# A macaron block on one core: the attention's table of steps made anew, with explicit lists for its first and last turns

## The chip, the cores and the metric

The kernel runs on one core of a Trainium2 chip. The metric is the device time of one execution in microseconds; the median over several runs is compared. The profile is of one execution, and its times are counted from the start of its span.

## What is computed

A block of three layers on `x` of shape (8, 1024, 256), float32: half a mixture-of-experts feed-forward layer, a memory layer called attention, and the same feed-forward layer again, each on the layer-normalised input and added to it.

```
x = x + 0.5 * ffn(layernorm(x))      # 8 experts, top-1, relu, weighted by the softmax
x = x + attn(layernorm(x))
x = x + 0.5 * ffn(layernorm(x))

# attn, for each batch row, in chunks of 128 tokens:
k, v, q = causal_conv4(x @ Wk.T), causal_conv4(x @ Wv.T), causal_conv4(x @ Wq.T)
alpha, eta, theta = means of sigmoid / sigmoid / softplus of three projections
g = grad of sum((silu(k @ W1.T) @ W2.T - v)**2) at the chunk's first W1, W2, clipped by its norm
S = eta_t * S - theta_t * g_t ;  W = (1 - alpha_t) * W + S        # for each token t
h = silu(q_t @ W1_t.T) ;  r_t = h @ W2_t.T
out = rmsnorm(r @ Wo.T) * norm_g * (x @ gW.T + gb)
```

The memory `W1, W2, S` goes from chunk to chunk, so that the eight chunks form a chain; all else of a chunk depends on its own tokens (and three tokens of the chunk before, for the convolution).

## The kernel before

The first expert layer, the attention and the second expert layer follow one another in `macaron`. In the attention a chunk `c` holds 128 tokens of all 8 batch rows, and there are `NC` = 8 chunks. The work of a chunk is cut into named steps, the methods of the class `Memory`. A step with `yield` in it comes in several pieces, one for each engine that it passes: `zk`, for instance, is a product on PE (L866), a sigmoid on ACT (L889) and a product on DVE (L891).

The pieces of a chunk, in the order of its data:

- The input. `load` (L640) fetches half of the rows through ACT's DMA queue into one of three buffers; `lx` (L645, DVE), `norm` (POOL, L627 to L653) and `xn` (L658, ACT) normalise them; `turn` (L665, L669) transposes them by PE and copies them by ACT.
- The projections, all on PE into two `pre` banks of PSUM. `ae` and `aem` give alpha and eta, `few` (L704, SP's queue) gathers them in eight rows, `prods` (L710, DVE) and `cut` (L719, POOL) finish these, and `spread` (L725 to L734, SP's queue) spreads them over the partitions by way of DRAM. `proj0`, `proj1`, `proj2` are k, v, q (L755; ACT copies L784, L787), `tap0` to `tap8` (L791, DVE) their convolution. `theta`, `soft`, `softplus`, `thm` give theta. `lt` and `ct` (L710, DVE) are the scans of the decay factors over time, 128 x 1024. `rows` transposes k and v, `qk` and `mq` (L850) weigh q by k.
- The gradient, which needs the chunk's memory. `zk` (L866, L889, L891) applies W1, `pred` (L876, L879, L866, L905) W2, `back` (L876, L879, L866, L912) goes back; `ds`, `sq`, `kn`, `both`, `clip` (L929 to L939, with a power on POOL, L95) give the clipped factor, `gc0` and `gc1` (L944, DVE) the scaled gradients.
- The next memory. `old0` to `old3` (L959 to L965, POOL) scale the old one, `step0`, `step1` (L977, PE) sum the gradients, `state` (L986, DVE) adds both, `by_out` (L995, L1004) transposes it.
- The output. `rq`, `hq`, `abh`, `hh`, `rh`, `rts` (L1014 to L1076) read the memory by q, `wide` (L1107, L1114) is the product with Wo and its squares, `rms` (POOL, L1121, L1122), `gate` (L1091, PE; L1099, ACT), `xo` (L1129, DVE), `add` (L1135, POOL, adds the residual row that `xr` fetched through ACT's queue, L1082), and `store` (L1140) sends two copies of 512 KB through ACT's queue. The output buffer `xo` exists twice, so a product of L1129 waits until the store that used its buffer two halves ago has left it.
- The routing of the second expert layer. `lo`, `std` (L102 to L107, POOL), `back_turn` (L1160, L1162), `logits` (L1169, L1179, L1182, L1185), and at the last chunk `choose`.

Every engine runs its instructions in the order in which the program issues them (`manual_schedule`), and that order is the table `ORDER`. A turn goes through the table once. `step-1` in it means that the step is done for the chunk before the one that the turn is named after, `step+1` for the chunk after it; a name that occurs again stands for the step's next piece. Turns before the first and after the last chunk use the same table and leave out what falls outside the eight chunks:

```
for turn in range(-max(offs), NC - min(offs)):
    for name, n, off in order:
        c = turn + off
        if not 0 <= c < NC:
            continue
```

In the table of before, the input of a chunk is turned and projected in the turn in which its `zk`, `pred` and `back` begin, `back` ends in the next turn (`rq-1`, `gc0-1`, `state-1`), and the outputs of a chunk come one and two turns later.

Of the kernel before, what the change touches and what calls it, by code (L numbers as in the profile page):

```python
# [1226 lines left out]

def attention(sh, i, x1, x2, out):
    nc, tc = sh.nc, sh.tc
    words = [re.fullmatch(r"([a-z_]+?)(\d*)([+-]\d)?", s).groups() for s in ORDER.split()]  # L1230
    order = [(name, int(n or 0), int(off or 0)) for name, n, off in words]
    offs = [off for _, _, off in order]
    with ExitStack() as st:
        mem = Memory(st, sh, i, x1, x2, out)
        begun = {}
        st.enter_context(tc.manual_schedule(engines=sh.engines))
        for turn in range(-max(offs), NC - min(offs)):
            for name, n, off in order:
                c = turn + off
                if not 0 <= c < NC:  # L1240
                    continue
                key = name, n, c
                if key in begun:
                    next(begun[key], None)
                    continue
                g = getattr(mem, name)(c, mem.u[c], n)
                if g is not None:
                    begun[key] = g
                    next(g, None)
# [72 lines left out]
```

## Time and profile before

| | |
|---|---|
| time, median of 3 runs | 820.73 us (820.3 to 824.27) |
| the profiled execution | 824.22 us, of which its span 822.4 us |
| mean granted PE clock | 0.927 |
| busy over the span: PE, DVE, ACT, POOL | 740.3, 453.8, 346.7, 470.6 us |
| the attention, first `xn` to last logit of the routing | 231.7 to 639.6 us |
| the state updates (L986), chunks 1 to 7 | begin at 284.7, 326.8, 373.7, 419.6, 466.1, 511.9, 561.8 us |
| the first product with the state (`zk`, L866), chunks 0 to 7 | begins at 252.4, 289.9, 331.6, 378.2, 424.0, 470.7, 516.5, 566.4 us |

Busy time is the union of an engine's records. PE's matmuls are pipelined and their ends are modelled, so that a PE that is busy all the time need not run at its peak. A line of a timeline gives the start in us, the duration in us (of a run of like instructions, from the first to the last), the engine, the line of the kernel, the operation with output and inputs, and in brackets how long the engine had been idle before it, and which producer ended that. A row of a table of stretches gives each engine's busy time in that stretch, the number of its instructions in brackets, then the granted PE clock (1.00 is full speed), the share of the DMA engines that was busy, and their GB/s. A line of the waits gives who waited for whom: us in total, times, and the longest.

### The profile page before, as it was taken

How to read it: one execution, taken by the hardware profiler on the slowest of the kernel's cores; microseconds unless marked ns; L12 is line 12 of the kernel's file. 1: busy time of each engine (PE TensorE's matmuls, PEld its weight loads, DVE VectorE, ACT ScalarE, POOL GpSimd, SP SyncE). 2: the span in 40 equal slices, each digit the busy share in tenths (PEclk: the TensorE clock that was granted, in tenths of full speed). 3: DMA queues.
4: the chain of work that ended last, by engine and by line, in shares of the span. 5: the costliest groups of instructions: out<-in, count | busy, mean ns of one | idle time of the engine just before them, and what ended most of it. 6: DMA issues, size and time to landing. Idle time of an engine off the chain costs nothing. (4 is left out here: it accounts for less than half of the span.)

```text
span 822.4 us, 13632 instructions
## 1 busy us (share of the span) xinstructions
PE 740.3 (90%) x5198; PEld 540.6 (66%) x5198; DVE 453.8 (55%) x931; ACT 346.7 (42%) x738; POOL 470.6 (57%) x610
## 2 busy tenths in 40 slices
PE   7869999999568999999999989999885599999996
PEld 5547777777426575766768575766663377777775
DVE  5862333220328988888887878868643534322310
ACT  3512222222047575767666676756433122222221
POOL 6625444531134768988888888875754354444411
PEclk9959999999867999999999999889968589999999
DMA  8995444540214242454454442334306824444420
GB/s 265 367 386 166 151 138 150 172 152 17 88 52 84 79 93 90 91 169 102 157 129 129 130 123 85 85 121 106 129 26 194 279 74 138 138 144 138 145 70 17
DMA packets 110945, 110.40 MB, mean 134 GB/s; under 512 B 12384, under 2 KB 103904, under 8 KB 110880
## 3 DMA queue, kind: packets, MB, share of 16 engines
q1 hardware_dynamic: 72528, 66.49, 27.1%
q10 hardware_dynamic: 32464, 31.47, 12.2%
q0 software_dynamic: 5888, 11.57, 4.3%
q8 instruction: 41, 0.67, 0.3%
q14 instruction: 24, 0.20, 0.1%
HBM read 78.80 MB, written 30.64 MB: 133 GB/s over the span
## 5 line engine op out<-in xcount | busy, mean ns | idle before, releaser
L352 ACT ACTIVATE hT<-ph 128x320 f32<-128x320 f32 x128 | 56.0, 437 | 225.5 <-PE ph L345 225.5
L345 PE MATMUL ph<-xT,w1t 128*128 128x320 f32 x512 | 149.5, 446 | 0.8 <-ACT xT L306 0.8
L345 PEld LDWEIGHTS ph<-xT,w1t 128*128 128x128 f32 x512 | 96.6, 194 | 41.9 <-issue 4.5
L373 DVE SCALAR_TENSOR_TENSOR xo<-py,gate,xg 128x256 f32<-128x256 f32 x32 | 15.5, 484 | 187.2 <-PE py L366 187.2
L366 PE MATMUL py<-w2t,hT 128*128 128x256 f32 x512 | 114.6, 382 | 0.0
L366 PEld LDWEIGHTS py<-w2t,hT 128*128 128x128 f32 x512 | 96.1, 190 | 13.7
L277 POOL DMA_INDIRECT gate<-gate_d,get x48 | 45.4, 945 | 33.8 <-DMA gate_d<-gates 19.8
L1091 PE MATMUL pre<-wg,xT 128*128 128x256 f32 x256 | 60.1, 394 | 2.5 <-DVE m L850 2.0
L755 PE MATMUL pre<-xT,w 128*64 128x512 f32 x256 | 61.4, 603 | 0.5 <-ACT kk L787 0.5
L1091 PEld LDWEIGHTS pre<-wg,xT 128*128 128x128 f32 x256 | 49.4, 196 | 11.1 <-DVE m L850 2.4
L1135 POOL TENSOR_TENSOR xo<-xo,xr 128x512 f32<-128x512 f32 x32 | 42.9, 1353 | 20.4 <-DVE xo L1129 20.2
L376 POOL DMA_INDIRECT x<-xo,put x16 | 16.0, 1002 | 54.3 <-DVE xo L373 45.8
L658 ACT ACTIVATE xt<-xt,ln_nm,lx_t 128x256 f32<-128x256 f32 x64 | 34.4, 593 | 25.0 <-POOL ln_nm L653 25.0
L376 POOL DMA_INDIRECT out<-xo,put x16 | 16.0, 1003 | 48.0 <-DVE xo L373 36.6
L1129 DVE SCALAR_TENSOR_TENSOR xo<-tail,rs,gate 128x256 f32<-128x256 f32 x64 | 27.1, 476 | 25.1 <-DMA out<-xo 16.2
L944 DVE TENSOR_TENSOR gc<-ehd,c 128x1536 f32<-128x1536 f32 x16 | 40.0, 2539 | 0.3
L755 PEld LDWEIGHTS pre<-xT,w 128*64 128x64 f32 x256 | 15.8, 136 | 30.4 <-issue 22.4
L665 PE MATMUL pre<-ident,xt 128*128 128x128 f32 x128 | 21.5, 303 | 15.5 <-ACT xt L658 14.1
L856 POOL TENSOR_TENSOR abq<-qq,ab 128x512 f32<-128x512 f32 x16 | 33.6, 2103 | 1.0 <-DMA ab<-kept 1.0
L678 PE MATMUL pre<-xT,w 128*128 128x512 f32 x64 | 32.6, 640 | 0.0
L389 PE MATMUL py<-w2t,hT 128*64 128x128 f32 x512 | 31.5, 276 | 0.0
L266 POOL DMA_INDIRECT xg<-hidden_in,get x24 | 23.6, 984 | 13.2 <-issue 6.7
(252 smaller groups left out, 1573.5 us busy)
## 6 DMA issues: line engine op xcount, KB each, us to landing
w1t<-w_in SPq DMA_DIRECT2D x16, 1024.0 KB
w2t<-w_in SPq DMA_DIRECT2D x16, 1024.0 KB
xt<-hidden_in SPq DMA_DIRECT2D x16, 512.0 KB
x<-xt SPq DMA_DIRECT2D x16, 512.0 KB
xt<-x ACTq DMA_DIRECT2D x16, 512.0 KB
xr<-x ACTq DMA_DIRECT2D x16, 512.0 KB
x<-xo ACTq DMA_DIRECT2D x14, 512.0 KB
out<-xo ACTq DMA_DIRECT2D x14, 512.0 KB
```

Of the source, the lines that this page charges most:

```text
L277: nc.gpsimd.indirect_dma_start(out=gate[:, s : s + 1], out_offset=None, in_=slots.gate, in_offset=bass.IndirectOffsetOnAxis(ap=slots.get[: ...
L345: nc.tensor.matmul(ph[:, :CAP], lhsT=a[:, c, f * P : (f + 1) * P], rhs=at[:, c, :], start=(c == 0), stop=(c == 1),)
L352: nc.scalar.activation(hT[:, f, :], ph[:, :CAP], AF.Relu)
L366: nc.tensor.matmul(py[:, :H], lhsT=hT[:, f, s * P : (s + 1) * P], rhs=b[:, f, :], start=(f == 0), stop=(f == FC - 1),)
L376: nc.gpsimd.indirect_dma_start(out=dst, out_offset=bass.IndirectOffsetOnAxis(ap=slots.put[:, e, s : s + 1], axis=0), in_=xo[:, s, :], in_o ...
L658: self.nc.scalar.activation(x, x, AF.Identity, bias=u.nm[:, j : j + 1], scale=u.r16[:, j : j + 1])
L678: self.nc.tensor.matmul(ps, lhsT=self.w3[:, k, 4 * D : 6 * D], rhs=u.xT[:, k, h * 512 : (h + 1) * 512], start=(k == 0), stop=(k == 1),)
L755: self.nc.tensor.matmul(ps[self.half[r], :], lhsT=self.w3[:, k, f * D : (f + 1) * D], rhs=u.xT[:, k].rearrange("h (p r t) -> h p r t", p=N ...
L856: self.nc.gpsimd.tensor_tensor(u.abq[:, n], u.kv[2], u.ab[:, n], ALU.mult)
L944: self.nc.vector.tensor_tensor(u.gc[:, layer], g.unsqueeze(2).to_broadcast([P, B, 3, D]), u.c3.rearrange("s n j -> s j n").unsqueeze(3).to ...
L1091: self.nc.tensor.matmul(ps[:, q * H : (q + 1) * H], lhsT=u.xT[:, k, j * P : (j + 1) * P], rhs=self.wg[:, k, :], start=(k == 0), stop=(k == 1),
L1135: self.nc.gpsimd.tensor_tensor(u.xo[h][:, two], u.xo[h][:, two], u.xr[h][:, two], ALU.add)
```

## The change

The table `ORDER` is made anew, with 163 entries instead of 165, and it is used for the middle turns only. Two lists, `FIRST` (398 entries) and `LAST` (393), name each step with its chunk (`zk@1`). A new function `steps` unfolds the table as before, replaces as many entries at its beginning as `FIRST` has by `FIRST`, and those at its end by `LAST`; both lists hold exactly the entries that they replace, in another order. The steps themselves are not changed. In the new table the input of a chunk is turned and projected in the turn before its `zk` (`turn0+1`, `proj0+1`), `back`, `clip` and `gc` fall in the chunk's own turn, and the output's second half comes at the start of the turn after next.

```diff
 ORDER = """
-choose0-2 gate0-2 xn3 store1-3 mq1-1 rms0-2 gate1-2 sq0-1 gate2-2 back-1 xo0-2 abq0-1 sq0-1 gate1-2 xo1-2
-xr1-2 gate3-2 sq2-1 both-1 gate2-2 turn0 turn0 ends-1 gate3-2 kn-1 rq-1 sq2-1 add0-2 turn1 old0-1
-turn3 turn1 add1-2 load1+1 back_turn0-2 turn2 clip-1 clip-1 lx1+1 turn3 turn2 ae0 back_turn1-2 ae0
-lx0+1 ae1 lo0-2 old1-1 lo1-2 back_turn0-2 back_turn1-2 ae1 old2-1 old3-1 proj0 clip-1 load0+2 gc0-1
-std0-2 gc1-1 aem logits0-2 lx2+1 proj0 proj0 aem logits0-2 hq-1 lx3+1 tap0 tap1 step1-1 logits0-2
-few tap2 logits0-2 norm+1 hq-1 hq-1 proj1 step0-1 xr0-1 proj1 prods cut abh1-1 wide1-2 proj1 theta
-state-1 wide1-2 tap3 hh-1 proj2 rms1-2 theta tap4 hh-1 xo2-2 abh0-1 theta xn0+1 proj2 zk add2-2
-proj2 xo3-2 tap5 rh-1 add3-2 zk rows1 soft tap6 rows1 zk softplus lo2-2 pred rows0 lo3-2 pred
-back_turn2-2 back_turn2-2 spread tap7 back_turn3-2 rts-1 back_turn3-2 rts-1 ds pred std1-2 tap8
-logits1-2 rows0 logits1-2 by_out-1 kept lt logits1-2 ksq sq1 logits1-2 choose1-2 thm pred thm wide0-1 back
-past+1 xn1+1 ds by_out-1 abq1 back qk wide0-1 ct back mq0 xn2+1 gate0-1 sq1 store0-2
+prods step0-1 tap0 step1-1 hq-1 proj2 tap1 tap3 tap4 xo3-2 theta cut proj2 theta xo2-2 norm+1 add3-2
+gate3-1 tap2 theta add2-2 state-1 hq-1 lo3-2 hh-1 tap5 by_out-1 tap6 abh0-1 hh-1 store0-2 tap7 gate3-1
+abh1-1 xr1-1 spread soft softplus back_turn3-2 back_turn2-2 xr0-1 back_turn3-2 back_turn2-2 lo2-2 std1-2
+rows0 rows1 tap8 lt zk logits0-2 rows0 logits0-2 by_out-1 zk logits1-2 rh-1 xn1+1 kept thm rts-1
+logits1-2 logits1-2 thm zk rows1 pred ds abq0 sq1 logits1-2 pred ct qk ds mq0 pred rts-1 xn0+1 wide0-1
+pred wide0-1 mq1 ends rms0-1 ksq sq1 xn2+1 gate0-1 gate0-1 old1 gate1-1 past+1 gate2-1 xn3+1 back
+gate1-1 gate2-1 back turn0+1 turn0+1 turn1+1 load1+2 lx0+2 back xo0-1 xo1-1 sq0 turn1+1 add0-1 kn
+turn2+1 add1-1 back_turn1-1 sq0 back turn2+1 turn3+1 back_turn0-1 ae0+1 sq2 both turn3+1 ae0+1 ae1+1
+back_turn1-1 sq2 ae1+1 abq1 clip rq old0 back_turn0-1 logits0-1 aem+1 store1-2 lo1-1 lx1+2 proj0+1
+logits0-1 aem+1 lx2+2 few+1 lo0-1 proj0+1 proj0+1 wide1-1 clip proj1+1 proj2+1 old2 wide1-1 std0-1 clip
+gc0 load0+3 old3 proj1+1 hq proj1+1 rms1-1 gc1 lx3+2
 """
+FIRST = """
...
+proj0@0 aem@0 lx1@1 lx2@1 proj0@0 tap0@0 norm@1 load1@2 aem@0 few@0 proj1@0 proj1@0 proj1@0 prods@0
+xn1@1 theta@0 tap3@0 proj2@0 tap1@0 xn2@1 tap2@0 theta@0 cut@0 tap4@0 proj2@0 theta@0 zk@0 xn0@1 kept@0
+tap5@0 zk@0 zk@0 turn1@1 proj2@0 tap6@0 tap7@0 spread@0 pred@0 xn3@1 ds@0 ds@0 old1@0 turn3@1 turn1@1
+pred@0 turn3@1 rows0@0 rows0@0 turn2@1 turn2@1 rows1@0 rows1@0 turn0@1 load0@2 tap8@0 pred@0 lt@0
+turn0@1 sq1@0 qk@0 ct@0 soft@0 past@1 ksq@0 mq0@0 old0@0 ae1@1 ae1@1 mq1@0 pred@0 proj1@1 back@0 sq1@0
+proj1@1 proj1@1 ae0@1 sq0@0 lx2@2 load0@3 proj0@1 ae0@1 lx1@2 tap3@1 back@0 proj0@1 kn@0 proj0@1 proj2@1
+back@0 proj2@1 lx3@2 abq1@0 aem@1 sq0@0 both@0 lx0@2 proj2@1 tap0@1 gate3@0 softplus@0 old2@0 back@0
...
+back@1 ds@1 turn1@2 back@1 sq0@1 xo1@0 turn3@2 sq0@1 turn1@2 load1@3 xo0@0 lx0@3 sq1@1 back@1
...
+clip@1 soft@2 tap0@2 tap1@2 clip@1 proj2@2 std0@0 proj2@2 rms1@0 gc0@1 gc1@1 store0@0 hq@1 xo2@0 old3@1
+add2@0 prods@2 xo3@0 step1@1 gate0@1 step0@1 proj1@2 lx3@3 hq@1 gate0@1 cut@2 proj1@2 add3@0 softplus@2
+tap6@2 hq@1 back_turn2@0 spread@2 thm@2 lx2@3 tap7@2 state@1 proj1@2 hh@1 lo3@0 back_turn3@0
...
+"""
+LAST = """
...
+back@7 ds@7 abq0@7 sq1@7 gate1@6 rms0@6 xo0@6 back@7 ds@7 back@7 ends@7 gate2@6 sq0@7 kn@7 sq0@7
+both@7 gate1@6 step0@7 add0@6 back@7 xo1@6 sq2@7 logits1@5 thm@7 sq2@7 gate2@6 add1@6 thm@7 clip@7
+logits1@5 lo1@6 store1@5 back_turn0@6 back_turn1@6 clip@7 back_turn0@6 lo0@6 back_turn1@6 wide1@6 rq@7
+wide1@6 store0@6 std0@6 rms1@6 clip@7 gc0@7 hq@7 xo3@6 gate0@7 xo2@6 add3@6 hq@7 hq@7 add2@6 gate1@7
+logits0@6 back_turn3@6 gc1@7 lo3@6 old3@7 abh0@7 logits0@6 back_turn3@6 back_turn2@6 by_out@7 lo2@6 hh@7
+back_turn2@6 by_out@7 xr0@7 abh1@7 hh@7 logits1@6 rh@7 gate0@7 logits1@6 rts@7 store1@6 logits0@6
+logits0@6 logits1@6 std1@6 rts@7 logits1@6 xr1@7 wide0@7 gate3@7 gate1@7 wide0@7 rms0@7 xo0@7 add0@7
+gate3@7 xo1@7 choose0@7 wide1@7 add1@7 lo1@7 gate2@7 wide1@7 rms1@7 gate2@7 xo3@7 kept@7 xo2@7
+back_turn0@7 add3@7 lo0@7 back_turn0@7 back_turn1@7 back_turn1@7 logits0@7 store0@7 add2@7 logits0@7
+back_turn2@7 back_turn3@7 back_turn2@7 logits0@7 std0@7 back_turn3@7 lo3@7 lo2@7 logits0@7 logits1@7
+std1@7 store1@7 logits1@7 logits1@7 logits1@7 choose1@7
+"""
+
+
+def steps():
+
+    turn_of = [re.fullmatch(r"([a-z_]+?\d*)([+-]\d)?", s).groups() for s in ORDER.split()]
+    turn_of = [(name, int(off or 0)) for name, off in turn_of]
+    offs = [off for _, off in turn_of]
+    plan = [
+        (name, turn + off)
+        for turn in range(-max(offs), NC - min(offs))
+        for name, off in turn_of
+        if 0 <= turn + off < NC
+    ]
+    first, last = ([(s.split("@")[0], int(s.split("@")[1])) for s in t.split()] for t in (FIRST, LAST))
...
+    a, b = len(first), len(plan) - len(turns)
...
+    return first + plan[a:b] + last
 
 
 def attention(sh, i, x1, x2, out):
...
-        for turn in range(-max(offs), NC - min(offs)):
-            for name, n, off in order:
...
+        for step, c in steps():
...
```

More of the change, by code (lines that the diff above doesn't have):

```diff
@@ new lines @@
+gc0 load0+3 old3 proj1+1 hq proj1+1 rms1-1 gc1 lx3+2
+"""
+FIRST = """
+load0@0 load1@0 lx1@0 lx2@0 lx3@0 load0@1 lx0@0 norm@0 xn1@0 xn0@0 turn1@0 xn2@0 xn3@0 turn0@0 turn1@0
+turn0@0 lx0@1 turn2@0 load1@1 past@0 turn2@0 turn3@0 lx3@1 ae0@0 turn3@0 xr0@0 ae1@0 ae0@0 proj0@0 ae1@0
+proj0@0 aem@0 lx1@1 lx2@1 proj0@0 tap0@0 norm@1 load1@2 aem@0 few@0 proj1@0 proj1@0 proj1@0 prods@0
+xn1@1 theta@0 tap3@0 proj2@0 tap1@0 xn2@1 tap2@0 theta@0 cut@0 tap4@0 proj2@0 theta@0 zk@0 xn0@1 kept@0
+tap5@0 zk@0 zk@0 turn1@1 proj2@0 tap6@0 tap7@0 spread@0 pred@0 xn3@1 ds@0 ds@0 old1@0 turn3@1 turn1@1
@@ new lines @@
+pred@0 turn3@1 rows0@0 rows0@0 turn2@1 turn2@1 rows1@0 rows1@0 turn0@1 load0@2 tap8@0 pred@0 lt@0
+turn0@1 sq1@0 qk@0 ct@0 soft@0 past@1 ksq@0 mq0@0 old0@0 ae1@1 ae1@1 mq1@0 pred@0 proj1@1 back@0 sq1@0
+proj1@1 proj1@1 ae0@1 sq0@0 lx2@2 load0@3 proj0@1 ae0@1 lx1@2 tap3@1 back@0 proj0@1 kn@0 proj0@1 proj2@1
+back@0 proj2@1 lx3@2 abq1@0 aem@1 sq0@0 both@0 lx0@2 proj2@1 tap0@1 gate3@0 softplus@0 old2@0 back@0
+sq2@0 sq2@0 aem@1 clip@0 abq0@0 tap1@1 gate3@0 few@1 thm@0 theta@1 clip@0 tap2@1 thm@0 ends@0 prods@1
@@ new lines @@
+gate0@0 cut@1 theta@1 clip@0 gc0@0 tap4@1 gc1@0 theta@1 rq@0 hq@0 norm@2 old3@0 hq@0 hq@0 step0@0 xn0@2
+lx1@3 gate1@0 step1@0 state@0 abh0@0 gate0@0 abh1@0 gate1@0 xn3@2 xn2@2 tap5@1 gate2@0 rows0@1 hh@0
+kept@1 tap6@1 rh@0 soft@1 rows0@1 hh@0 tap7@1 zk@1 ksq@1 tap8@1 rts@0 gate2@0 rows1@1 spread@1 by_out@0
+softplus@1 zk@1 old0@1 lt@1 zk@1 rts@0 old1@1 thm@1 abq0@1 pred@1 ct@1 rows1@1 thm@1 by_out@0 xn1@2 qk@1
+pred@1 abq1@1 wide0@0 pred@1 past@2 mq0@1 turn0@2 mq1@1 wide0@0 pred@1 kn@1 rms0@0 turn0@2 turn2@2
@@ new lines @@
+turn2@2 back@1 ds@1 turn1@2 back@1 sq0@1 xo1@0 turn3@2 sq0@1 turn1@2 load1@3 xo0@0 lx0@3 sq1@1 back@1
+sq1@1 ds@1 turn3@2 ends@1 ae0@2 ae1@2 add1@0 add0@0 ae0@2 back@1 sq2@1 xr1@0 lo1@0 proj0@2 load0@4 ae1@2
+both@1 sq2@1 proj0@2 back_turn0@0 back_turn1@0 clip@1 old2@1 proj0@2 back_turn1@0 theta@2 lo0@0
+back_turn0@0 logits0@0 theta@2 aem@2 logits0@0 wide1@0 xr1@1 rq@1 aem@2 wide1@0 theta@2 few@2 proj2@2
+clip@1 soft@2 tap0@2 tap1@2 clip@1 proj2@2 std0@0 proj2@2 rms1@0 gc0@1 gc1@1 store0@0 hq@1 xo2@0 old3@1
@@ new lines @@
+add2@0 prods@2 xo3@0 step1@1 gate0@1 step0@1 proj1@2 lx3@3 hq@1 gate0@1 cut@2 proj1@2 add3@0 softplus@2
+tap6@2 hq@1 back_turn2@0 spread@2 thm@2 lx2@3 tap7@2 state@1 proj1@2 hh@1 lo3@0 back_turn3@0
+back_turn2@0 abh0@1 gate3@1 abh1@1 logits0@0 tap2@2 rh@1 xr0@1 gate3@1 back_turn3@0 norm@3 thm@2 hh@1
+xn1@3 kept@2 lo2@0 rows0@2 rows0@2 zk@2 xn0@3 logits1@0 std1@0 rts@1 tap8@2 logits1@0 tap3@2 tap4@2
+logits0@0 logits1@0 by_out@1 lt@2 rts@1 ct@2 qk@2 zk@2 xn3@3 ends@2 logits1@0 wide0@1 old1@2 zk@2 ds@2
@@ new lines @@
+pred@2 ksq@2 wide0@1 pred@2 mq0@2 lx0@4 ds@2 mq1@2 gate2@1 sq1@2 xn2@3 tap5@2 gate1@1 gate2@1 gate1@1
+rms0@1 kn@2 sq1@2 rows1@2 abq0@2 pred@2 by_out@1 xo0@1 rows1@2 turn1@3 add0@1 pred@2 turn2@3 back@2
+turn1@3 turn0@3 sq0@2 past@3 back@2 load1@4 turn0@3 xo1@1 back@2
+"""
+LAST = """
+lo0@4 state@7 logits0@4 lx3@7 old0@7 wide1@4 wide1@4 clip@5 clip@5 proj0@6 old2@5 lx2@7 gc1@5 gc0@5
+step1@5 aem@6 norm@7 few@6 proj1@6 proj0@6 proj0@6 tap0@6 theta@6 tap1@6 rms1@4 proj1@6 proj1@6 hq@5
+prods@6 tap3@6 std0@4 xn0@7 theta@6 cut@6 tap4@6 tap2@6 theta@6 proj2@6 proj2@6 hq@5 step0@5 old3@5
@@ new lines @@
+xo3@4 xo2@4 proj2@6 gate2@5 xn2@7 hq@5 logits0@4 gate3@5 state@5 store0@4 tap5@6 gate2@5 hh@5 soft@6
+tap6@6 logits0@4 add3@4 add2@4 rows1@6 xr0@5 gate3@5 rows1@6 lo3@4 xn1@7 hh@5 by_out@5 spread@6
+back_turn3@4 back_turn3@4 abh1@5 back_turn2@4 rows0@6 abh0@5 xr1@5 tap7@6 zk@6 back_turn2@4 rh@5
+logits1@4 tap8@6 zk@6 lo2@4 softplus@6 store1@4 lt@6 rows0@6 zk@6 thm@6 rts@5 logits1@4 by_out@5 thm@6
+pred@6 kept@6 logits1@4 ct@6 qk@6 std1@4 old0@6 pred@6 pred@6 old1@6 logits1@4 sq1@6 mq0@6 past@7 pred@6
@@ new lines @@
+rts@5 wide0@5 mq1@6 xn3@7 wide0@5 ksq@6 gate1@5 sq1@6 sq0@6 gate1@5 sq0@6 gate0@5 gate0@5 turn0@7 kn@6
+ds@6 back@6 turn0@7 rms0@5 xo0@5 step1@7 turn3@7 turn1@7 back@6 turn3@7 xo1@5 old2@6 back@6 turn1@7 ds@6
+turn2@7 both@6 turn2@7 back@6 ae0@7 sq2@6 ae0@7 add1@5 add0@5 proj0@7 proj0@7 back_turn1@5 lo1@5
+back_turn0@5 ends@6 proj0@7 back_turn0@5 sq2@6 ae1@7 clip@6 back_turn1@5 clip@6 ae1@7 wide1@5 aem@7
+wide1@5 store0@5 lo0@5 aem@7 tap0@7 abq1@6 proj2@7 clip@6 gc0@6 few@7 abq0@6 gc1@6 proj1@7 rq@6 rms1@5
@@ new lines @@
+old3@6 prods@7 proj1@7 proj1@7 hq@6 xo3@5 proj2@7 xo2@5 step1@6 tap3@7 tap1@7 cut@7 proj2@7 add3@5
+add2@5 step0@6 std0@5 gate3@6 hq@6 logits0@5 gate3@6 hq@6 theta@7 xr1@6 old1@7 tap2@7 back_turn3@5
+tap4@7 lo3@5 state@6 tap6@7 logits0@5 back_turn3@5 theta@7 hh@6 theta@7 rows0@7 abh1@6 back_turn2@5
+logits0@5 tap7@7 abh0@6 hh@6 back_turn2@5 tap8@7 spread@7 zk@7 rh@6 lo2@5 xr0@6 logits1@5 rows0@7 tap5@7
+std1@5 rows1@7 rts@6 zk@7 zk@7 lt@7 logits0@5 soft@7 logits1@5 softplus@7 rows1@7 rts@6 pred@7 pred@7
@@ new lines @@
+sq1@7 qk@7 wide0@6 pred@7 by_out@6 ksq@7 ct@7 mq0@7 mq1@7 wide0@6 by_out@6 gate0@6 pred@7 gate0@6 abq1@7
+old2@7 back@7 ds@7 abq0@7 sq1@7 gate1@6 rms0@6 xo0@6 back@7 ds@7 back@7 ends@7 gate2@6 sq0@7 kn@7 sq0@7
+both@7 gate1@6 step0@7 add0@6 back@7 xo1@6 sq2@7 logits1@5 thm@7 sq2@7 gate2@6 add1@6 thm@7 clip@7
+logits1@5 lo1@6 store1@5 back_turn0@6 back_turn1@6 clip@7 back_turn0@6 lo0@6 back_turn1@6 wide1@6 rq@7
+wide1@6 store0@6 std0@6 rms1@6 clip@7 gc0@7 hq@7 xo3@6 gate0@7 xo2@6 add3@6 hq@7 hq@7 add2@6 gate1@7
@@ new lines @@
+back_turn2@7 back_turn3@7 back_turn2@7 logits0@7 std0@7 back_turn3@7 lo3@7 lo2@7 logits0@7 logits1@7
[12 more added lines that the diff above has]
+    first, last = ([(s.split("@")[0], int(s.split("@")[1])) for s in t.split()] for t in (FIRST, LAST))
+    turns = [s for s in last if not s[0].startswith("choose")]
+    a, b = len(first), len(plan) - len(turns)
+    assert sorted(first) == sorted(plan[:a]) and sorted(turns) == sorted(plan[b:])
+    return first + plan[a:b] + last
@@ L1228, in attention @@
 def attention(sh, i, x1, x2, out):
     nc, tc = sh.nc, sh.tc
-    words = [re.fullmatch(r"([a-z_]+?)(\d*)([+-]\d)?", s).groups() for s in ORDER.split()]
-    order = [(name, int(n or 0), int(off or 0)) for name, n, off in words]
-    offs = [off for _, _, off in order]
     with ExitStack() as st:
@@ L1236, in attention @@
         st.enter_context(tc.manual_schedule(engines=sh.engines))
-        for turn in range(-max(offs), NC - min(offs)):
-            for name, n, off in order:
[L1239 to L1249, printed above, removed]
+        for step, c in steps():
+            if (step, c) in begun:
+                next(begun[step, c], None)
+                continue
+            name, n = re.fullmatch(r"([a-z_]+)(\d*)", step).groups()
+            g = getattr(mem, name)(c, mem.u[c], int(n or 0))
+            if g is not None:
+                begun[step, c] = g
+                next(g, None)
 @with_exitstack
```

## The prediction, made before the changed kernel was run

> **What bounds the kernel now.** I read the cores first (one core, 822.4 us), then stretches of the span by engine, then the waits of the attention's middle turns, then the timeline of its end. The attention runs from the first normalisation at 231.7 us to the last routing logit at 639.6 us: 407.9 us. The expert phases on both sides are not touched.
>
> ```profile
> L986 DVE TENSOR_TENSOR st<-core,go x7: 1186/1186/1186, 284.7 to 561.8; 128x1024 f32<-128x1024 f32 x7
> ```
> The state update, once a chunk: six turns in 277.1 us, 46.2 us each.
>
> ```profile
> core 0: us, PE busy (x) PEld busy (x) DVE busy (x) ACT busy (x) POOL busy (x), PEclk, DMA share, GB/s
> 232.00:253.00 21.00, 18.94 (x70) 8.27 (x72) 5.55 (x12) 13.86 (x25) 3.52 (x11) 0.75 0.17 51
> 253.00:267.00 14.00, 11.88 (x85) 10.57 (x84) 13.04 (x14) 10.95 (x21) 8.75 (x8) 0.61 0.58 115
> 374.00:420.00 46.00, 43.73 (x410) 30.70 (x407) 39.16 (x62) 31.57 (x67) 39.39 (x48) 1.00 0.45 127
> 562.00:598.00 36.00, 31.20 (x322) 23.46 (x318) 29.20 (x45) 20.34 (x47) 29.27 (x31) 0.99 0.42 118
> 598.00:640.00 42.00, 29.27 (x196) 21.06 (x195) 16.61 (x38) 13.21 (x39) 20.67 (x34) 0.74 0.39 126
> ```
> A middle turn (third row) is full on three engines at once. In the last 42 us no engine is (DVE 40%, POOL 49%, PE long records at a clock of 0.74): there the order of the steps, not work, sets the time. The head (first rows) has a slow clock and a half-idle DVE.
>
> ```profile
> DVE xo L1129 <- DMA out<-xo: 9.3, 4, 2.5
> PE core L876 <- DVE ehd L891: 4.9, 5, 1.1
> PE tail L1107 <- DVE dl_b L1185: 2.9, 5, 0.6
> ```
> The waits between 327 and 561 us: small, about 1 us of PE here and there. And the end:
>
> ```profile
> 588.38 0.88 DVE L1129 SCALAR_TENSOR_TENSOR xo<-tail,rs,gate 128x256 f32<-128x256 f32 x2 [4.16 <-DMA out<-xo]
> ...
> 620.98 1.66 DVE L1129 SCALAR_TENSOR_TENSOR xo<-tail,rs,gate 128x256 f32<-128x256 f32 x4 [2.69 <-DMA out<-xo]
> ...
> 632.06 1.66 DVE L1129 SCALAR_TENSOR_TENSOR xo<-tail,rs,gate 128x256 f32<-128x256 f32 x4 [4.32 <-POOL rs L1122]
> ```
> The output product waits for a store to leave its buffer, or for the step ahead of it: chunk 6's and chunk 7's ends run one behind the other.
>
> **The change part by part.** Nothing is added or removed: the lists hold the same steps of each chunk in another order, so that it does something else is excluded. SP's transfers (few, spread) keep their order among themselves. So I count work issued ahead of a landmark, each step at its row (a projection or gate pair on PE 1.75 us, a group of four transposes 0.44, a tap 0.74, gc 2.65, lt and ct 2.28 and 2.57, an add on POOL 1.38, a std 4.6, and so on). A turn sums to PE 40.7, DVE 39.7, POOL 39.0 us. Landmark: zk of chunk c (L866, first use of its state), us of PE / DVE / POOL ahead of it.
>
> - zk0: 13.0/11.3/8.7 in both. Before: at 252.4 us.
> - zk2: before 77.4/80.5/61.7 at 331.6 us; after 85.0/82.9/65.9.
> - zk3: before 118.1/120.2/100.7 at 378.2; after 122.1/127.8/109.3.
> - zk5: before 199.6/199.6/178.7 at 470.7; after 203.5/207.2/187.3.
> - zk6: before 240.3/239.3/217.7 at 516.5; after 246.1/243.3/220.4.
> - zk7: before 281.0/275.8/252.5 at 566.4; after 284.1/279.6/255.2. All: 323.4/316.4/306.2, at 639.6 us.
>
> *First list, up to zk2.* prods now stands between tap0 and tap1, tap2, and waits for the few transfer (landed 250.8 to 251.4), so zk0 slips by about 2.3 us to 254.7. Then chunk 1's projections are put between chunk 0's pred and back: 15.2 us of PE instead of 5.6 from zk0 to the end of dh0. That end goes from 266.5 to about 274, gc's from 278.4 to 287, state0 from 284.7 to 289.6, zk1 from 289.9 to 293.4. From there the fill is already done: dz1 at 308.3, then clip 1.0+1.65+0.43, gc 5.3, and on DVE xo2, prods, xo3, two lx, two taps, hq (6.9) put state1 at 327 (before 326.8) and zk2 at 332. Equal time, with 7.6 us of PE and 2.4 of DVE more done.
>
> [...] The row: granted clock 0.61 from 253 to 267. [...]
>
> *Middle turns*, only 3.2 of them now (from add1 of chunk 1 to lx1 of chunk 7). Counted from start to start of its groups of matmuls, the turn 373.7 to 419.6 is 43.0 us of PE work and 2.9 us of gaps: 1.1 ahead of pred's transposes (hk), 0.7 inside wide0 (dl), 0.9 ahead of the gates (m), rest 0.2. In the new table dl comes earlier (gap gone); zk to pred has rh, thm, rts and logits between (4.4 us), while hk is now queued on DVE behind tap8 and lt: 0.4 left; gate0 behind mq0 0.5. New: hh waits for hq, which stands behind prods, five taps, two xo and state on DVE: 0.9; back_turn1 waits for add1 on POOL: 0.7. Sum 2.5 instead of 2.9: about 45.5 us a turn, nothing much. The store wait goes (stores are now issued some 10 us ahead of the xo that reuses the buffer; ACT issues as many DMAs, and xr1 now holds ACT until add2, about 0.5 us, covered by soft's slack); late next is the gate copy behind osq, ksq and xn2 on ACT. The table load moves from ae's sigmoid to zk's, which is on the chain of the state: 1.28 us (row L686 load), covered by zk's own 1.0 us on PE and by lt on DVE; uncovered it would be 1.3 us a turn. spread now follows cut behind std0, old3 and rms1 on POOL; kept to eta took 5.9 us in the head (252.5 to 258.4), and there are about 12 us till lt: 6 us of slack.
>
> [...] The row: a tiny POOL step, 0.2 us at 609, takes 2.84 beside the eta scan:
>
> ```profile
> 385.29 2.84 POOL L103 TENSOR_TENSOR lo_t<-lo_st 128x4 f32<-128x4 f32 x1
> 385.85 2.28 DVE L710 TENSOR_TENSOR_SCAN eta<-eta,diag 128x1024 f32<-128x1024 f32 x1
> ...
> 609.34 0.20 POOL L103 TENSOR_TENSOR lo_t<-lo_st 128x4 f32<-128x4 f32 x1
> ```
> [...]
>
> From zk2, then: zk2 to zk3 holds 44.9 us of DVE and 43.4 of POOL, 5 more than a turn, so 49 us: zk3 at 381 (+2.8). Two turns of 45.7: zk5 at 472.5 (+1.8).
>
> *Last list.* To zk6 42.6 of PE: 46 us, 518.5. To zk7 38.0 of PE, times 43.0/40.7 and 2.5 of gaps: 42.5, so 561 (before 49.9 us, 566.4). From the end of dh7 I lay chunk 7's chain through the new queues, before in brackets (from 582.0): gc0 done 7.5 (14.4, behind chunk 6's xo and lo and a 4.2 us store wait); hq 13.3, behind std0, rms1, xo3 and xo2 of chunk 6 (18.1); m2 17 (22.6); rts 20.5 (31.0); first xo 25 (40), since gates 0, 1 and 3 are done in earlier waits instead of as 7 us after rts; choose0's 4.1 us then sits between xo1 and lo1, partly beside wide1, osq and rms1; last xo 33 (51.7); last dl 38.3 (57.6). Zk7 to dh7 is 14.5 (15.6). That is 53 against 73.2; the same hand sum of a middle turn falls 2.3 of 43 short, and waits will be missed, so I take 57. End at 618, 21.6 us earlier. The second expert phase starts from the last choose, as before.
>
> The profiled execution took 824.2 us (span 822.4 and 1.8 around it): 824.2 − 21.6 = 802.6; it lies 3.5 above the median of the runs, so 799.
>
> **The rivals.**
> - *Only the end gains (811).* dh0 is late by the row's clock (+7 not recovered) and the rest of chunk 7's chain keeps 5 us more of waits. For: head's walk adds 7.6 us to a chain before it pays. Against: from zk1 on the work is already done.
> - *More (789).* The middle and the turns around it come to the 43 us floor: 3 us less in three or four turns. Against: three engines at 85 to 95%.
> - *No change (821).* The head's fill is not paid back (10 us, half clock and zk0's slip together) and each of six turns is 2 us longer.
> [...]
>
> **How the numbers follow.** Both list gains as walked 0.55; only the end 0.24; more 0.08; no change 0.05; slower 0.08. A measurement tells about 0.5%, 4 us, from no change: faster 0.87, same 0.05, slower 0.08. The likeliest, 799, holds 791 to 808 alone; 787 leaves about one in ten below, 815 one in ten above.
>
> **What would show it.** Right: state updates still about 46 us apart in the middle, the seventh 5 us earlier; zk2 near 332; clock above 0.8 from 255 to 275; no xo waiting for a store; last dl about 57 us behind zk7. Wrong: state updates 48 us or more apart with POOL records stretched; dh0 past 280; DVE idle before lt for eta; the end over 65 us behind zk7.

## The result, and the profile after

The changed kernel took 830.99 us (829.31 to 833.43, 7 runs) beside 823.96 us of the kernel before (820.3 to 826.66, 7 runs): a ratio of 1.0107 (1.0073 to 1.0141). It is 1.1% slower; 799 us and a gain were predicted. The profiled execution took 829.31 us (before 824.22), so the two traces differ by 5.1 us, the medians by 7.0.

Stretches of the changed kernel by engine. The columns are length, the busy time of PE, weight loads, DVE, ACT and POOL with their instruction counts, then the granted PE clock. The first four stretches are those shown of before.

```profile
core 0: us, PE busy (x) PEld busy (x) DVE busy (x) ACT busy (x) POOL busy (x), PEclk, DMA share, GB/s
232.00:253.00 21.00, 17.22 (x58) 7.75 (x60) 2.92 (x8) 13.26 (x23) 4.30 (x15) 0.72 0.25 76
253.00:267.00 14.00, 9.21 (x80) 7.01 (x76) 13.44 (x15) 12.25 (x23) 4.25 (x4) 0.88 0.68 153
374.00:420.00 46.00, 41.92 (x391) 31.15 (x389) 34.37 (x59) 28.92 (x62) 32.54 (x45) 0.93 0.42 125
562.00:598.00 36.00, 32.60 (x339) 22.68 (x337) 30.47 (x36) 20.88 (x47) 27.25 (x28) 1.00 0.42 104
598.00:645.00 47.00, 38.10 (x301) 28.29 (x301) 27.43 (x55) 17.91 (x47) 30.77 (x47) 0.82 0.41 135
```
The head has the clock that was forecast (0.88 against 0.61 before) and the end is packed more tightly. The middle stretch is the surprise: DVE, ACT and POOL are all *less* busy in it than before (34.4, 28.9 and 32.5 us against 39.2, 31.6 and 39.4), and the clock is 0.93 and not 1.00. Some of that is fewer instructions (59 of DVE and 45 of POOL against 62 and 48); in whole turns with nearly equal counts, shown below, they are less busy as well. So the middle waits.

The state update, for the line of it shown before:

```profile
L986 DVE TENSOR_TENSOR st<-core,go x7: 1201/1218/1227, 295.3 to 579.8; 128x1024 f32<-128x1024 f32 x7
```
The first comes 10.6 us later than before and the last 18.0 us later. The end of the last chunk, in the timeline of DVE:

```profile
610.93 1.66 DVE L1129 SCALAR_TENSOR_TENSOR xo<-tail,rs,gate 128x256 f32<-128x256 f32 x4 [2.89 <-POOL rs L1122]
...
629.35 1.66 DVE L1129 SCALAR_TENSOR_TENSOR xo<-tail,rs,gate 128x256 f32<-128x256 f32 x4 [5.36 <-POOL rs L1122]
...
636.50 1.64 DVE L1129 SCALAR_TENSOR_TENSOR xo<-tail,rs,gate 128x256 f32<-128x256 f32 x4
...
645.19 0.19 DVE L1185 TENSOR_TENSOR dl_b<-tail,r_b 128x32 f32<-128x32 f32 x1 [1.58 <-PE tail L1182]
```
No output product waits for a store any more. The last logit ends at 645.4 us, 60.7 us behind chunk 7's `zk`. Laid against the forecast, by the first product with the state:

| stretch | before | forecast | after | missed by |
|---|---|---|---|---|
| start of zk0 | 252.4 | 254.7 | 256.2 | +1.5 |
| zk0 to zk3 | 125.8 | 126.3 | 132.0 | +5.7 |
| zk3 to zk5 | 92.5 | 91.5 | 97.3 | +5.8 |
| zk5 to zk7 | 95.7 | 88.5 | 99.2 | +10.7 |
| zk7 to the last logit | 73.2 | 57.0 | 60.7 | +3.7 |

The five misses sum to 27.4 us, which is the end at 645.4 against the forecast 618. From `zk0` to the last logit the changed kernel takes 389.2 us and before 387.2.

### The profile page after: what moved, and what is told of

It is laid out like the page before. It is cut to its first block, busy times and chain, and to the rows that moved or that the text cites. A ratio compares the mean times of both kernels' runs of the same rounds, so it can differ in the third digit from the quotient of the medians.

```text
span 827.5 us, 13680 instructions
## 1 busy us (share of the span) xinstructions
PE 735.3 (89%) x5198; PEld 536.5 (65%) x5198; DVE 443.4 (54%) x931; ACT 346.3 (42%) x738; POOL 459.9 (56%) x610
## 5 line engine op out<-in xcount | busy, mean ns | idle before, releaser
L1091 PE MATMUL pre<-wg,xT 128*128 128x256 f32 x256 | 64.1, 399 | 2.8 <-ACT gate L1099 1.9
L1091 PEld LDWEIGHTS pre<-wg,xT 128*128 128x128 f32 x256 | 48.0, 195 | 17.7 <-issue 4.9
L1135 POOL TENSOR_TENSOR xo<-xo,xr 128x512 f32<-128x512 f32 x32 | 40.8, 1286 | 10.2 <-DVE xo L1129 7.7
L665 PE MATMUL pre<-ident,xt 128*128 128x128 f32 x128 | 21.5, 307 | 17.3 <-ACT xt L658 16.2
L645 DVE BATCH_NORM_STATS2 lx_st<-xt 128x6 f32<-128x256 f32 x64 | 22.9, 410 | 15.3 <-DMA xt<-x 15.3
L389 PEld LDWEIGHTS py<-w2t,hT 128*64 128x64 f32 x512 | 27.6, 137 | 5.3 <-issue 5.3
```

Of the source, the lines that this page charges most:

```text
L389: nc.tensor.matmul(py[h * D : (h + 1) * D, :P], lhsT=hT[:, f, 2 * P :], rhs=b[:, f, h * P : (h + 1) * P], start=(f == 0), stop=(f == FC - ...
L1091: self.nc.tensor.matmul(ps[:, q * H : (q + 1) * H], lhsT=u.xT[:, k, j * P : (j + 1) * P], rhs=self.wg[:, k, :], start=(k == 0), stop=(k == 1),
L1135: self.nc.gpsimd.tensor_tensor(u.xo[h][:, two], u.xo[h][:, two], u.xr[h][:, two], ALU.add)
```

## The experiments

Ratios below are against the kernel before, run beside each kernel on the same chip. Four chips were used, and the kernel before differs between them: 822.51 us beside e1 to e4, 821.85 beside e5 to e8, 835.83 beside e9 to e12 and 833.13 beside f1 to f4, with mean granted clocks of 0.928, 0.929, 0.920 and 0.922. So kernels of different chips are compared by their ratios, or by stretches inside their traces. The one trace of the kernel before is that of the 824.22 us run.

**The parts alone.** Each kernel takes the steps of a list out of the unfolded table and puts the list in their place (in words, not the code itself):

```diff
+    plan = [s for s in unfolded table of before, less the entries of LAST]
+    return plan + last                      # e1; e2: first + plan, less FIRST
```


> The table of before for all steps, with the last list alone in place of the steps that it holds; the first list and the new table are not used. Theory (the parts add up, the end's gain is the last list's own): the walk from chunk 7's read of the state to the last logit goes from 73.2 us to about 61, as in the changed kernel, and chunks 1 to 5 stand as before, so 812 to 815 against 824. Rival (the end's gain needs the work that the new table and the first list had done ahead): the last list finds less done and gives it back at its start, 821 to 827. The ACT wait for the ab transfer (15.0 us in the middle turns of the changed kernel) is absent before the last list.

> The first list alone, then the table of before to the end. Theory (the first list itself costs: ae of chunk 1 waits for a bank, old3 of chunk 0 stands behind norm of chunk 2, clip behind taps): chunk 2's read of the state comes 11 to 15 us later than before, and no more than 5 of it are paid back by the work done ahead, so 832 to 838 against 824. Rival (the slip is only work done ahead, and comes back by the third chunk): 822 to 826.

> The new table alone from the first to the last turn, without the two lists. Theory (the new table has an ACT wait of about 5 us in every turn, of which some 2 us are not covered, and its own ends are not good): turns of 48 us in the middle, and an end that is longer than the 60.6 us of the last list, so 835 to 850. Rival (the lists are what costs, the table is as good as before's): 820 to 826.

The last list alone: 812.19 us, ratio 0.9882 (0.9855 to 0.991). The first list alone: 829.23, ratio 1.0088 (1.0054 to 1.0122). The new table alone (`return plan + choose`): 849.27, ratio 1.0334 (1.0306 to 1.0362). So the end is gained by the last list itself, 59.7 us from zk7 to the last logit; the first list costs, though less than the 832 to 838 us that were expected; and the new table is the worst of the three parts, with its own head and end in that figure (66.3 us from zk7 to the last logit). The two lists alone would add up to 0.997, so that some 1.4% of the changed kernel's 1.0107 is left for the new table between them. With the last list alone the steps from zk5 to zk7 take 101.3 us instead of 95.7, at the same 10.2 us of half clock, as gate products (72 matmuls of L1091 against 64) and other work of later turns are done there, and this is paid back at the end.

**The wait of ACT in the middle turns.** Between 388 and 538 us the waits of the changed kernel begin with a line that before does not have, and ACT's timeline shows where:

```profile
ACT sp L805 <- DMA ab<-kept: 15.0, 3, 6.5
```
```profile
478.80 0.52 ACTq L1140 DMA_DIRECT2D out<-xo  x1
...
480.24 0.59 ACT L1099 COPY gate<-pre 128x512 f32<-128x512 f32 x1 [0.65 <-PE pre L1091]
486.65 0.37 ACTq L1082 DMA_DIRECT2D xr<-x  x1
487.35 0.63 ACT L805 ACTIVATE sp<-sp 128x512 f32<-128x512 f32 x1 [6.52 <-DMA ab<-kept]
```
The sigmoid does not read `ab`. In the trace the 258 transfers issued on SP's and ACT's queues name one of eight completion counters each (semaphores 100 to 107, 32 or 33 transfers to a counter). This issue waits for 104, which is its own too. The last transfer with 104 is the eighth issue back, the seven between having one each of the other seven: an `ab` of the same chunk's `spread`, issued on SP at 477.96; its last piece landed at 486.63 us, and `xr` was issued at 486.65. The add that frees the buffer of `xr`, which the prediction named, had ended at 482.1. ACT stands at the issue and everything queued behind it stands too. The obvious test is to take the issue off ACT:

```diff
-        self.nc.scalar.dma_start(u.xr[h], self.x1[c, :, NP * h : NP * (h + 1), :])
+        self.nc.sync.dma_start(u.xr[h], self.x1[c, :, NP * h : NP * (h + 1), :])
```


> The changed kernel with one edit: the load of the residual rows (xr) is issued on SP's queue and not on ACT's. Theory (xr's issue stands at the head of ACT's queue until the ab transfer, issued eight transfers before it, has landed, and soft, zk's sigmoid and eta's scan are queued behind it): ACT's wait of 15.0 us in three turns goes, middle turns fall from 48 to 49 us to 46, and the time falls by 5 to 10 us, to 821 to 826. [...] Second rival (xr only waits for the add that frees its buffer, and something else is late next): under 2 us gained.

833.1 us, ratio 1.0126 (1.0098 to 1.0155). The wait is gone from the list, and nothing is gained: as the cause of the time that theory fell. The waits between 388 and 545 us now begin so:

```profile
DVE dl_b L1185 <- PE tail L1182: 19.2, 3, 7.7
POOL ends L749 <- DVE ct L710: 15.9, 3, 6.6
```
PE is what the others wait for now, and its timeline says why:

```profile
497.90 1.08 PE L1169 MATMUL tail<-xrT,gwc 128*32 128x128 f32 x16 [3.34 <-DVE dl_b L1185]
498.91 3.68 PE L1014 MATMUL core<-abh,st 64*64 64x128 f32 x32
...
504.31 1.97 PE L1028 MATMUL core<-m,gc 128*64 128x128 f32 x16
```
PE stands 3.34 us for the bank that `dl` frees, behind the 2.28 us scan of eta on DVE. After it the 16 products of L1028 take 1.97 us, where 16 of them took 1.04 at 481.5 us: half clock. Two edits, alone and with `xr` moved:

```diff
-rows0 rows1 tap8 lt zk logits0-2 rows0 logits0-2 by_out-1 zk
+rows0 rows1 tap8 zk logits0-2 rows0 logits0-2 lt by_out-1 zk
```


> The changed kernel with the residual rows on SP's queue, and in the table the scan of eta (lt) behind the first half's last logits step (dl) on DVE. Theory (two waits stand one behind the other in the new table: ACT at xr's issue, and PE at the bank that dl frees behind the 2.3 us scan of eta; with the first one gone PE still stood 3.3 us and its clock was halved for 10 to 14 us): only with both gone do the middle turns fall to 45 to 47 us from 48 to 55, and the time to 819 to 826. [...]

> The changed kernel with the scan of eta behind dl, and xr still on ACT's queue. Theory (two waits in series): PE still stands 3 to 4 us for the transposed rows (xrT) that are queued on ACT behind xr's issue, and its clock is still halved, so 828 to 834, within 3 us of the changed kernel. Rival (dl behind the scan was the only one that counts): 820 to 826.

Both together: 828.97, ratio 1.0081 (1.0054 to 1.0108). That is just below the 829 to 835 us expected if work itself sets the middle turn, and it is not clear of the changed kernel's 1.0107. The scan moved alone: 833.37, ratio 1.0116 (1.0077 to 1.0155), nothing, as its theory of two waits in series had it. That each wait hid the other is therefore not shown; a turn was still 50.9 or 47.9 us.

**What the turns have in common.** Turns of one table differ by their clock. These are stretches from one chunk's `zk` to the next: first three of before (the last has the slowest clock of its turns), then the two middle turns of the changed kernel, then one of the kernel with both edits.

```profile
331.60:378.20 46.60, 45.01 (x408) 32.08 (x406) 39.11 (x62) 31.38 (x66) 39.34 (x48) 0.96 0.44 123
378.20:424.00 45.80, 43.52 (x408) 30.70 (x406) 38.95 (x62) 31.38 (x66) 39.32 (x48) 1.00 0.45 128
...
516.50:566.40 49.90, 48.37 (x410) 34.40 (x408) 36.98 (x54) 30.64 (x64) 35.16 (x38) 0.90 0.34 97
```
```profile
388.20:437.70 49.50, 45.42 (x408) 32.60 (x408) 36.11 (x62) 32.33 (x68) 35.68 (x47) 0.93 0.41 118
437.70:485.50 47.80, 44.31 (x406) 31.81 (x406) 36.21 (x62) 30.45 (x65) 36.48 (x47) 0.96 0.41 123
```
```profile
391.10:442.00 50.90, 46.94 (x406) 34.10 (x406) 37.04 (x62) 31.30 (x67) 37.06 (x48) 0.90 0.38 114
```
A clock of 0.93 over 49.5 us is 6.8 us at half rate (twice 0.07 of the length), 0.96 is 3.4, and 0.90 is 10.2: always a multiple of 3.4 us. In the traces of before and of the changed kernel the granted clock is either 1.00 or 0.50, and each stretch of the one or the other, but for the last, is a whole multiple of 3.41 us long (1 to 47 times). At most half of that is lost, and half of it taken off each turn of the new table leaves 46.1, 46.1 and 45.8 us. The true price is smaller where waits shrink beside slower products: in before the turns with one such window are 0.8 and 0.9 us longer than the clean ones (46.6 and 46.7 against 45.8), not 1.7, and the one with three is 4.1 longer. PE's own records say what the clock did in the changed kernel. The matmuls of its two turns take 45.42 and 44.31 us; those of the same steps take 42.32 us in a turn of 45.7 us at full clock (e12, below). Of the 5.9 us that the two turns are longer than two of those, 5.1 are longer records of PE. So what they lack is mostly the clock. Where the clock falls, seen at the step of the windows, before and in the changed kernel:

```profile
430.10:433.50 3.40, 3.40 (x63) 2.79 (x63) 3.40 (x4) 2.30 (x5) 3.40 (x2) 1.00 0.04 7
433.50:436.90 3.40, 2.82 (x30) 2.25 (x27) 1.55 (x4) 2.57 (x7) 3.09 (x8) 1.00 0.02 5
436.90:440.30 3.40, 3.40 (x22) 2.51 (x22) 2.78 (x1) 1.62 (x6) 3.40 (x2) 0.50 0.00 0
```
```profile
387.10:390.50 3.40, 1.11 (x16) 0.97 (x16) 3.40 (x6) 2.15 (x3) 1.05 (x1) 1.00 1.14 303
390.50:393.90 3.40, 2.47 (x27) 1.76 (x29) 1.92 (x2) 3.38 (x6) 2.89 (x4) 0.50 0.81 252
393.90:397.30 3.40, 3.40 (x30) 3.07 (x26) 1.38 (x2) 1.74 (x5) 3.19 (x6) 0.50 0.02 5
```
In the changed kernel PE is idle for two thirds of the window ahead of the fall. In before it is *busy* for 2.82 of 3.40 us and the clock falls all the same: that window holds products of 64 by 64, a transpose and products of two columns. I weighted the columns that each matmul of the traces streams by the rows and columns it uses, as shares of 128 by 128 (the largest form in these traces), and summed that by window; the sums are an estimate, good for comparing windows. Before's window at 433.5 us holds 1158 columns so weighted. In the traces of before and of the changed kernel there are 145 windows at full clock between 330 and 600 us; the 9 that are followed by half clock hold 282 to 1170 such columns, and the other 136 hold 1473 or more. Of the 1335 such windows in the eighteen traces (of before, of the changed kernel and of the sixteen experiments), 56 are followed by half clock. A bound at about 1390 columns sorts all but 7; without the weight by rows and columns the best bound leaves about 30.

That is a correlation. The test is to give the array a little work there: three transposes, which `thm` overwrites at once. By the weighting they add 384 columns to the 1158 of before's window at 433.5 us. If it is the array's weighted work that counts, the half windows between 330 and 560 us (17 us in the trace of before) go, and the time falls to 814 to 819 us; if the windows are only a sign of waits that cost the same anyway, it is 821 to 825.

```diff
         ps = self.pre()
+        for _ in range(3):
+            self.nc.tensor.transpose(ps[:, :P], self.sh.ident, self.sh.ident)
         for p in range(NP):
```


> The kernel before, with three more transposes of the identity (0.11 us of PE each, written over at once by the step itself) at the head of thm, where the array does little: 16 matmuls of 64x64, one transpose and 8 matmuls of two columns in 3.4 us. [...]

> The last list alone on the table of before, with the same three transposes in thm. Theory (as for the kernel before so filled): the half windows at 386 and 478 us (13.6 us in the trace of the last list alone) go, 804 to 809. Rival (no cost of its own): 811 to 815.

```profile
336.30:382.10 45.80, 43.83 (x411) 31.02 (x409) 39.03 (x62) 31.41 (x66) 39.65 (x48) 1.00 0.47 127
...
519.70:565.60 45.90, 43.94 (x413) 31.05 (x411) 37.26 (x54) 30.43 (x64) 35.03 (x38) 1.00 0.37 105
```
```profile
437.40:440.80 3.40, 3.14 (x35) 2.60 (x31) 1.55 (x4) 2.62 (x7) 3.09 (x8) 1.00 0.02 5
440.80:444.20 3.40, 2.94 (x38) 2.30 (x37) 3.29 (x2) 2.26 (x9) 3.40 (x2) 1.00 0.00 0
```
Kernel before with *more* work: ratio 0.9853 (0.9813 to 0.9893), 823.72 us beside 835.83. All five turns from zk2 to zk7 are 45.8 or 45.9 us at a clock of 1.00, where the trace of before has 45.8 to 49.9; the last two lines show the place where before's clock fell, and it stays at 1.00. From `zk0` to the last logit the two traces have 378.1 and 387.2 us. Of these 9.1 us, 5.5 lie in the five turns, which held five half windows: 1.1 us each. What makes up the rest of the 12.1 us between the medians is open: on this chip the kernel before ran at a lower clock, and it was not traced there. The filled last list: ratio 0.978 (0.9742 to 0.9818), and 0.9815 (0.9767 to 0.9864) when it was run once more (f4); it is the best version found, below both kernels.

> As the filled last list, and the residual rows on SP's queue. Theory (in the last list one issue of xr holds ACT for some 4.6 us while the transposed rows of chunk 5 wait behind it): 2 to 4 us below the filled last list. Rival (that wait is covered, as it was in the middle turns where taking it away gained nothing): within 1.5 us of it, or above.

With `xr` on SP as well it is no better: 0.9832 (0.9784 to 0.9879). So the ACT wait in the last list shows no cost of its own either.

**The new table at full clock.** What keeps PE idle round `zk` in it stands in the timelines of PE and DVE, here of the changed kernel:

```profile
388.21 1.11 PE L866 MATMUL core<-st,kk 64*128 64x64 f32 x16 [1.40 <-DVE m L1064]
391.42 0.48 PE L1182 MATMUL tail<-ident,lt 128*128 128x128 f32 x1 [2.10 <-ACT xrT L1162]
```
```profile
384.27 1.07 DVE L791 SCALAR_TENSOR_TENSOR vv<-raw,cw,vv 128x512 f32<-128x512 f32 x1
385.26 1.76 DVE L791 SCALAR_TENSOR_TENSOR qq<-raw,cw,qq 128x512 f32<-128x512 f32 x1
386.94 1.21 DVE L1064 TENSOR_TENSOR m<-core,ct 128x1024 f32<-128x1024 f32 x1
```
A tap that takes 0.74 us elsewhere takes 1.76 beside POOL's `abh` (384.74 to 388.15), the product of `hh` comes behind two lengthened taps, and `zk` waits 1.4 us for the bank that it frees. With `xr` off ACT (e3) that wait stands there all the same, 1.42 us. So, with `xr` on SP:

```diff
-... lo3-2 hh-1 tap5 by_out-1 tap6 abh0-1 hh-1 ...  tap8 lt zk logits0-2 rows0 logits0-2 by_out-1
+... lo3-2 hh-1 tap5 hh-1 by_out-1 tap6 abh0-1 ...  zk logits0-2 rows0 logits0-2 tap8 lt by_out-1
```


> The changed kernel with xr on SP's queue and in the table two products moved forward on DVE: m2 (hh's second step) ahead of tap6, and dl ahead of tap8 and eta's scan. Theory (what keeps PE idle round zk in the new table is DVE: m2 and dl stand behind taps that take 1.8 us instead of 0.74 beside POOL's abh and softplus, 1.4 and 1.9 us of PE idle, and the half clock that follows): middle turns at 45 to 47 us, 819 to 824. Rival (some other order in the table is late next): 826 to 831.

```profile
400.30:446.00 45.70, 42.32 (x408) 30.50 (x406) 37.21 (x62) 31.52 (x67) 39.51 (x48) 1.00 0.45 127
446.00:492.90 46.90, 44.00 (x409) 31.99 (x408) 37.17 (x62) 31.24 (x67) 37.56 (x48) 0.96 0.43 126
```
Ratio 0.9969 (0.994 to 0.9997): from 1.1% above before to 0.3% below, with the same lists. As the two ratios are not against the same runs of before, the traces are the better evidence: from `zk0` to the last logit 379.4 us, against 389.2 of the changed kernel. The middle turns are 45.7 and 46.9 us, one half window is left in them, and zk3 to zk7 takes 185.4 us instead of 196.5. This is the turn that was forecast. It comes when PE's idle time round `zk` falls from 3.5 us (1.40 and 2.10) to 1.60; which of the three moves (`xr`, the product of `hh`, `dl`) does it was not taken apart.

**The first list.** Four orders in it looked bad in the trace: chunk 1's `ae` waits 2.6 us for a bank that `qk` holds, the state update 2.6 us for `old3` behind `norm`, `clip` and `gc` of chunk 0 stand behind taps of chunk 1, and chunk 0's `prods` stands ahead of two of its taps.

```diff
-... qk@0 ct@0 ... mq0@0 ... ae1@1 ae1@1 mq1@0 ... tap1@1 ... prods@1 ... clip@0 gc0@0 ... norm@2 old3@0
+... ct@0 ... ae1@1 ae1@1 ... ae0@1 qk@0 mq0@0 mq1@0 ... clip@0 gc0@0 gc1@0 tap1@1 tap2@1 prods@1 ... old3@0 norm@2
```


> The first list, mended, then the table of before to the end. Mended: prods of chunk 0 behind its taps 1 and 2; qk and mq of chunk 0 behind chunk 1's ae and projections (so that ae finds a bank); clip and gc of chunk 0 ahead of chunk 1's taps and prods on DVE; old3 of chunk 0 ahead of norm of chunk 2 on POOL. Theory (these four orders made the 15 us): chunk 2's read of the state at 333 to 338 us instead of 346.6, and 816 to 824 in all, as 10 of the 15 us came back by the third chunk anyhow. Rival (the head is late because chunk 1's projections stand ahead of chunk 0's end, at a half clock): 826 to 832 as with the first list alone.

> The mended first list, the table of before in the middle, and the last list. Theory (the parts add up): 812.2 of the last list alone, plus what the mended first list does to the table of before (it alone against before, run beside this one), so 805 to 815. Rival (the last list's gain is the work ahead that the first list has taken already): 818 to 824.

Neither came: 1.01 (1.005 to 1.0151) and 0.9998 (0.9976 to 1.0021). The two waits are gone from the trace, and others stand in their place (DVE's `mq` 5.4 us for the moved `qk`, PE 2.7 us for a gate's copy), so that zk0 to zk3 took 132.3 us instead of 128.6; and a turn of 50.3 us with three half windows came on top, beside the one of 49.9 us that the first list alone has too. With the three transposes in `thm`:

> The first list, then the table of before, filled by the three transposes in thm. The filled kernel before was 1.5 per cent below before. Theory (the first list's own cost is 5 us, of which 2.3 is the slip of chunk 0's read and the rest is work put ahead of chunk 0's end that no turn pays back): 0.7 to 1.1 per cent below before. Rival (its cost was only the place of the half windows): 1.5 per cent below, as without it.

> The new table mended (xr on SP's queue, m2 and dl ahead of the taps) and filled (three transposes in thm), the last list, and no first list. Theory (the first list costs about 5 us wherever it stands, the mended table turns in 45.5 to 46 us with the clock held): 1.5 to 2.5 per cent below before, 5 us or more below f3. Rival (the new table needs the first list to start well; without it its first turns are 45 and 53 us, as in the table alone): no better than f3.

> The changed kernel with the table mended (xr on SP's queue, m2 and dl ahead of the taps) and three transposes in thm. Unfilled it was 0.3 per cent below before. Theory (one half window of 3.4 us was left in its middle turns and some in the head): 0.5 to 1 per cent below before. Rival (the filling only costs, 0.33 us in each of 8 turns): 0 to 0.3 per cent below.

> The last list on the table of before, filled by three transposes in thm, once more beside the others. It was 2.2 per cent below before on another chip. Theory: 1.8 to 2.6 per cent below again, and the best of the four unless f1 reaches it.

The first list on the filled table of before: 0.9971 (0.9934 to 1.0007), against 0.9853 without it. From zk3 on its turns are at a clock of 1.00, and both traces have 10.2 us of half clock ahead of that, so its cost is its own and not only the place of the half windows. By these ratios it is about 1.2%, more than the 5 us that were expected. On the mended new table it makes no difference: 0.9957 (0.9923 to 0.999) with it, 0.9961 (0.9924 to 0.9997) without, where 1.5 to 2.5% below before was expected without it. The filling did little for that table, 0.9957 against 0.9969: the half windows left in its middle turns follow windows at `zk`, and not at `thm`.

## Why the prediction was wrong

- **Middle turns (45.5 us each; 48.7 on average).** The failed step is the sum of 43.0 us of PE work and 2.5 of gaps: it has no term for the clock. I had read the clock of one turn of before, 374 to 420, and it is one of the two in five without a half window; the others have 0.96, 0.96 and 0.90. The size of the sum was about right: at full clock the mended turn is 45.7 us (e12), though the table as forecast never ran at full clock. In the changed kernel the two turns hold 10.2 us at half clock, and the longer records of PE make 5.1 us; 5.8 us were missed. The clock falls where PE is idle 1.4 us ahead of `zk` and up to 2.1 behind it; I had counted 2.5 us of gaps in a whole turn and not asked how close together they lie.
- **"xr1 now holds ACT until add2, about 0.5 us".** It held ACT 5.0 us a turn, and for another transfer than the add's buffer. That step was wrong by ten times; but "covered by soft's slack" was right in effect, since freeing ACT gained nothing by itself.
- **The clock in the head (dh0 at about 274; 280.2).** The 274 counts chunk 1's added products at about full clock; that they bring the clock back was my estimate, and no run shows it. What the changed kernel shows is 0.88 from 253 to 267 us, better than the 0.61 of before, with half windows at 257.4 and at 267.6 us, and the last product of dh0 on PE ends at 280.2 us. I took the clock for a matter of stretches that look slow, and did not ask what it does to a denser table. How much of the time PE is busy does not settle it either: its records fill 2.82 of 3.40 us at 433.5 us in before, and the next window is at 0.50 all the same. By the weighting above small products count for little; with three transposes more the clock stayed at 1.00 there (e9).
- **zk5 to zk7 (88.5; 99.2).** 10.2 us at half clock again, at most 5.1 us. The mended table does it in 92.8 us at full clock, so 4.3 us were missed by the walk. The other 6.4 are 4.0 of longer records of PE (89.5 us against 85.4) and 2.4 of waits.
- **First list (zk2 at +0.4; it was +14.8).** Its slip of zk0 (forecast 254.7; 254.7 with the first list alone, 256.2 in the changed kernel) is of the size forecast, though zk0 alone differs by 2.4 us between two executions with the head of before. What failed is "the fill is already done", the term that made the added work free: from zk0 to zk2 I summed 72.0 us of PE work into 77.3, and it took 90.2; before needs 79.2 for 64.4. There was little room: PE's records fill 74.1 of those 79.2 us in before, part of it at half clock. In the changed kernel they fill 82.3 of 90.2, so the added products came on top, and PE's idle time grew by 2.9 us besides. 7.2 us of it came back from zk2 to zk3 (41.8 us against 49 forecast). Which order in the list makes the remaining cost is open: mending the four named above did not take it away.
- **The end (57; 60.7).** Right in mechanism, no store wait, and 12.5 of the 16.2 us were had. The walk lacked waits such as the 5.4 us for `rs` at 629 us, and it had no term for the clock here either (0.82 from 598 to 645 us); what each cost was not measured.
- **The slower outcome (0.08).** It came, but without the stretched POOL records that the prediction names beside longer turns at its end: in a turn with equal counts of DVE (62) and one POOL instruction less both were busy for less (36.1 and 35.7 us against 39.0 and 39.3). Single taps are stretched beside POOL (1.76 us for 0.74), and PE waits behind them; what stretches them was not tested.

## What to carry to other kernels

Read the granted clock of every turn, not of one, before a table of steps is changed: on this kernel one 3.4 us window at half clock made a turn 0.8 to 1.2 us longer and three made it 4.1 longer, and the turns of one table fell into it three times in five (before), each time (the changed kernel's two middle turns) or never (e9). Where PE's work is thin for some 3 us, three transposes whose result is thrown away may be worth more than a better order: they gave 1.5% to the kernel before, and next to nothing to the mended table, where the thin place was another. And a long wait in a list is not yet a price: take it away alone, and see what is late next.

## What was not expected of the hardware

- The clock fell to half after windows in which PE was busy for over 80% of the time (2.82 of 3.40 us) with small products. A bound at about 1390 on the columns streamed in a window, weighted by the array's rows and columns in use, sorts 1328 of 1335 windows of these traces; that sum is an estimate from the matmuls' shapes.
- Adding 0.33 us of PE work to each of eight turns made the kernel before 1.5% faster (1.1 to 1.9%).
- An issue on ACT's queue kept ACT idle for up to 6.5 us until a transfer of SP's queue had landed whose data it does not use: the issue waits for semaphore 104, one of the eight (100 to 107) that the 258 transfers of the two queues name, and was made at 486.65 us, when that transfer's last piece had landed at 486.63.
